# The last two output projections of a two-layer attention kernel: one moved behind the last attention, the last one rebuilt from block and quarter products

## The chip, the cores and the metric

The kernel runs on one core of a Trainium2 chip. The metric is the device time of one execution in microseconds (us). Beside it there is one profiled execution, whose records give the start and length of every instruction on every engine: TensorE (PE, its weight loads PEld), VectorE (DVE), ScalarE (ACT), GpSimd (POOL) and the queue of SyncE (SP), which issues the DMA transfers.

## The reference

Two layers of the same form are applied to x of shape (8, 512, 32, 32), all in float32. With N = 1024 positions and C = 512 channels, for each image:

```python
xn = group_norm(x) * gamma + beta              # 8 groups in layer 0, 32 in layer 1
q, k, v = split(qkv_w @ xn + qkv_b)            # each 512 x 1024, 8 heads of 64
p = softmax(q.T @ k / 8)                       # per head, 1024 x 1024
out = p @ v.T                                  # per head, back to 512 x 1024
x = proj_w @ out + proj_b + x                  # output projection and residual
```

## The kernel before

**Units.** A unit is one image in one layer: units 0 to 7 are layer 0, units 8 to 15 layer 1. For each unit `fast_path` issues, in program order: the q, k and v projections (`projections`), then the output projection of the unit before (`project(old, after)`, L1163), then its own attention (`attention`, L1207). So the softmax tail of a unit is worked off beside the next unit's projections, and its output projection stands between the next unit's projections and attention. Unit 15 has no next unit: its output projection is `project_last` (L759, called in L1220).

**Order.** Nothing is planned by costs: every engine works through its instructions in the order in which the program issues them, and waits are put in by data dependence (and by `gate`, a TensorE instruction that waits for named others). Work of other units is threaded in through numbered calls: in `projections` and `project` every step ends in a call `done`, and a table says which parts are issued at which call.

**Products.** `blocks` (L422) multiplies two 2x2 block matrices with seven block products instead of eight. A block product is four matrix products of 512 columns. For some of the seven, each is made again from seven quarter products of 256 columns (`inner_products`, L437, `mix_inner`, L187). For the output projection, products 2, 3 and 4 are of that kind (`INNER["o"]`), 1, 5, 6 and 7 plain. Each needs sums and differences of blocks of the right operand (`mix_right`, L167), and of the left one, which is prepared once per layer (`left_o`, and for the quarters `inner_left` in DRAM).

The order of one projection, with its `done` calls: product 1, copied by ScalarE to p1 (call 1); product 6, added by VectorE to p1, giving u2 (call 2, in which VectorE also adds bias and residual to u2); quarter group 2, then `c11`, the first result block (call 3); product 7, its sum u3 (call 4, residual into u3); product 5, `others(1,1)` (call 5, residual into p1); quarter group 4, `others(1,0)` (call 6); quarter group 3, `others(0,1)` (call 7). In a quarter group ScalarE copies four of the seven results out of their banks (L460): quarter products 1, 6 and 7 of a group go into one bank one after the other, each one added to the last, and each is copied before the next. GpSimd then sums these copies (`fold`, L466) and adds them to the results (`rests`, L741), which are stored.

**Attention.** 64 steps: 8 chunks (4 pairs of heads by 2 halves of the positions) of 8 steps. A step is eight score products (L820), an exponential on ScalarE (L828) into one of four `p` buffers, a row sum on VectorE (L865, L867) and eight products with v (L848). At the end of a pair the row sums are transposed, reduced and sent through DRAM to become reciprocals `rb` for all rows (`reciprocals`, L901); VectorE multiplies with them (`divide`, L928) and ScalarE adds v's bias (`add_bias`, L935). For the last pair of a unit this lies behind attention.

**The last projection** has none of the mixing: for eight result tiles it multiplies the first three of four pieces (24 products of 512 columns), issues the last pair's reciprocals, division and bias, then the fourth pieces, each followed by one VectorE instruction and a store.

**Buffers.** `ppool` has four buffers `p`, `accpool` two `acc`, `trpool` two `tr`, `tmppool` one `tmp`, `rbpool` one `rb`; TensorE's results are in four two-bank tiles: `sbank[0]`, `sbank[1]` ("s" in the profile), `apair[0]`, `apair[1]` ("a").

Of the kernel before, what the change touches and what calls it, by code (L numbers as in the profile page):

```python
# [11 lines left out]
F32 = mybir.dt.float32  # L12
I32 = mybir.dt.int32
AF = mybir.ActivationFunctionType
ALU = mybir.AluOpType
# [3 lines left out]
P = 128  # L19
# [13 lines left out]
def fast_path(ctx, tc, x, qkv_wT, proj_wT, vecs, groups, out, flag):  # L33
# [55 lines left out]
    turns = [t[:, i, :] for i in range(2) for t in (*sbank, *apair)]  # L89
# [33 lines left out]
    def load_xn(u):  # L123
        t = xnpool.tile([P, CC, N], F32, tag="xn", name=f"xn_{u}")
        load_x(u, [t[:, c, :] for c in range(CC)])
        return t
# [37 lines left out]
            lefts.append({1: a11, 2: a12, 3: s4, 4: a22, 5: s1, 6: s2, 7: a21})  # L164
        return lefts, parts

    def mix_right(name, low, high):  # L167


        b11, b12 = low[:, :, :FD], low[:, :, FD:]  # L170
        b21, b22 = high[:, :, :FD], high[:, :, FD:]
        factors = {1: b11, 2: b21, 3: b22, 7: b12}

        def part(i):
            if i == 0:
                for k, n in ((5, 1), (6, 2), (4, 4)):
                    factors[k] = tpool.tile([P, 2, FD], F32, tag=f"{name[0]}{n}", name=f"{name}_t{n}")
            t1, t2, t4 = (factors[k] for k in (5, 6, 4))
            nc.vector.tensor_sub(
                *((t1, b12, b11), (t2, b22, t1), (t4, b21, t2), (b12, b22, b12))[i]  # L180
            )

        return factors, [partial(part, i) for i in range(4)]
# [77 lines left out]
    def load_proj(l, tag):  # L261
        w = wpool.tile([P, CC, C], F32, tag=tag, name=f"wproj_{l}_{tag}")
        nc.sync.dma_start(w, proj_wT[l].rearrange("(c p) o -> p c o", p=P))
        return w
# [155 lines left out]
                )  # L420

    def blocks(name, left, right, tokens, c11, others, done, u3_in, summed, inner={}, rests=None,  # L422
               u2_in=(trpool, "tr"), between=None, behind=None, p1=None):

# [38 lines left out]
                step(j)  # L463
            return (rest, partial(step, order[-1])) if k == 1 else rest

        def fold(rest):  # L466
            add = nc.gpsimd.tensor_add
            add(rest[:, 0, FD2:], rest[:, 0, FD2:], rest[:, 1, FD2:])  # L468
            add(rest[:, 1, FD2:], rest[:, 1, :FD2], rest[:, 1, FD2:])

        def add_rest(r, h, rest, alone=None):

            if rest is not None:
                fold(rest)
                rests(r, h, rest, alone)
# [52 lines left out]
        done(sums)  # L528
        rest = inner_products(bz, 3)
        others(0, 1, bz, u2, twice)  # L530
        add_rest(0, 1, rest, u2 if twice is not None else None)
        if twice is not None:
            rests(0, 1, twice)
        done(sums)
# [157 lines left out]
        if not w.v_first:  # L692
            values()

    def project(w, after):


        l, b = units[w.u]
# [39 lines left out]
                if (r, h) == (1, 1):  # L738
                    store(o, h)

        def rests(r, h, rest, _):  # L741
            for i in range(2):
                o = 2 * r + i
                cols = results[o, h]
                nc.gpsimd.tensor_add(cols, cols, rest[:, i, :])
                store(o, h)

        w.evac = [None, None]
# [4 lines left out]
        }  # L753
        inner = {k: (*w.inner_o[k], *plan[k]) for k in w.inner_o}
        w.taken = blocks(
            f"o_{w.u}", w.left, w.right_o, False, c11, others, done, (rbpool, "rb"), plain_sum, inner, rests
        )

    def project_last(w, rest):  # L759

        l, b = units[w.u]
        dst = mid[b] if l == 0 else out[b]

        def products(g, c):
            o, h = divmod(g, NH)
            nc.tensor.matmul(  # L766
                turns[g], w.wproj[:, c, ts(o, P)], w.ao[c // 2][:, c % 2, ts(h, FD)],
                start=(c == 0), stop=(c == CC - 1),
            )

        for g in range(CC * NH):
            for c in range(CC - 1):
                products(g, c)
        for part in rest:
            part()
        for g in range(CC * NH):
            o, h = divmod(g, NH)
            products(g, CC - 1)
            cols = w.res[o][:, ts(h, FD)]
            nc.vector.scalar_tensor_tensor(  # L780
                cols, turns[g], vec[:, l, PB, o : o + 1], cols, ALU.add, ALU.add
            )
            nc.sync.dma_start(dst[o * P : (o + 1) * P, ts(h, FD)], cols)

    def attention(w, at_step, at_end):


        u = w.u
        w.ao = [
            aopool.tile([P, 2, N], F32, tag=f"ao{i}", name=f"ao_{u}_{i}") for i in range(2)  # L790
        ]
# [183 lines left out]
        def bias_last():  # L975
            for h in range(NH):
                add_bias(CC - 1, h)

        w.right_o, mixing = mix_right(f"o_{u}", *w.ao)

        parts = {
# [7 lines left out]
        lefts = []  # L989

        def load_left():
            n = 2 * FD // P
# [11 lines left out]
        def mix_o(k):  # L1004
            tag = {2: "x2", 3: "x1", 4: "x4"}[k]
            room = tpool.tile([P, 4, FD2], F32, tag=tag, name=f"ro{k}_{u}")
            if k == INNER["o"][-1]:
                w.inner_o[k] = mix_inner_in(w.right_o[k], room, nc.vector)
                lefts.append(room[:, 3, :P])
                if u == B:  # L1010
                    make_left(2)
                else:
                    nc.sync.dma_start(lefts[-1], src[:, len(lefts) - 1, :])
            else:
                w.inner_o[k], subs = mix_inner(w.right_o[k], room, nc.vector)
                for part in subs:
                    part()
# [10 lines left out]
        w.finish = finish  # L1028
        return parts


    xn = xnpool.tile([P, CC, N], F32, tag="xn", name="xn_0")
    tiles = [xn[:, c, :] for c in range(CC)]
# [33 lines left out]
    for u in range(2 * B):  # L1067
# [54 lines left out]
        if old is not None:  # L1122
            old.res = load_res(old.u)
        nxt = None
        if u + 1 < 2 * B:
            xn = load_xn(u + 1)
            nxt = norm_parts(u + 1, xn)
            right, mixing = mix_right(f"x_{u + 1}", xn[:, :2], xn[:, 2:])
            for transfer in behind_loads:
                transfer()  # L1130
            behind_loads.clear()
        else:
# [70 lines left out]
        def at_end():  # L1203
            if u + 1 < 2 * B:
                w.made_next = load_inner_left(u + 1)

        rest = attention(w, at_step, at_end)  # L1207
        old = w

    both = const.tile([P, 1], F32, name="both")  # L1210
# [10 lines left out]
    nc.tensor.matmul(turns[0][:1, :1], both, ones[:, :1], start=True, stop=True)  # L1221
    nc.scalar.copy(flag, turns[0][:1, :1])


def general_path(ctx, tc, x, qkv_wT, proj_wT, vecs, groups, out):
# [260 lines left out]
```

## Time and profile before

| | us |
|---|---|
| time of the kernel before, median of 3 runs (range) | 3257.72 (3256.99 to 3259.81) |
| span of the profiled execution | 3256.9 |
| TensorE busy | 3244.5 |
| VectorE busy | 2715.3 |
| ScalarE busy | 1650.2 |
| GpSimd busy | 1216.3 |
| end of unit 15's q, k, v projections on the chain | 3089.74 |
| first scores of the last attention | 3112.54 |
| end of the last attention's products | 3222.57 |
| end of the last projection's products | 3250.27 |

A line of a timeline gives the start and the length in us, the engine, the line of the program, the operation, what it writes and reads by the program's names, the shape, and how many such instructions were merged. In brackets stands how long the engine had been idle before, and what ended that. The chain of work that ended last is followed back from the last instruction: at each step to what released it, or to the instruction before it on its engine. A float32 matrix product appears as two records.

### The profile page before, as it was taken

To read this page: it belongs to the slowest core of one execution; us is meant where nothing else is said; L and a number is where in the kernel's file an instruction comes from. 1 tells how busy PE (TensorE), PEld (TensorE's weight loads), DVE (VectorE), ACT (ScalarE), POOL (GpSimd) and SP (SyncE) were. 2 spreads that over 40 slices of the span, in tenths; PEclk is the share of its full clock that TensorE was granted. 3 is DMA by queue.
4 is the path that set the end of the run, shared out by engine and by line. 5 is a ranking of instruction groups with operands and counts; after the bars stand their busy time and mean duration, and the time that the engine had idled before them with its cause. 6 is when DMAs were issued, how large, how long until landed. Compare 5 with 4: busy or idle time off the path is not lost.

```text
span 3256.9 us, 56805 instructions
## 1 busy us (share of the span) xinstructions
PE 3244.5 (100%) x22206; PEld 1863.3 (57%) x22206; DVE 2715.3 (83%) x3488; ACT 1650.2 (51%) x2296; POOL 1216.3 (37%) x1207
## 2 busy tenths in 40 slices
PE   9999999999999999999999999999999999999999
PEld 5465474654746547465574655747556474564743
DVE  5887978789787897989979889797897978979786
ACT  1653626546274463744637446373563735637354
POOL 2054171531706317063270732607126071350710
PEclk9999999999999999999999999999999999999999
DMA  3112120121201212023120121201212012120111
GB/s 104 48 45 79 46 79 28 45 79 46 85 22 45 85 43 86 18 71 114 55 87 27 45 86 46 85 16 45 86 46 85 17 54 76 46 85 22 67 71 48
DMA packets 86463, 192.51 MB, mean 59 GB/s; under 512 B 22960, under 2 KB 34992, under 8 KB 84272
## 3 DMA queue, kind: packets, MB, share of 16 engines
q1 hardware_dynamic: 86192, 188.82, 17.0%
q8 instruction: 180, 2.95, 0.4%
q14 instruction: 91, 0.75, 0.1%
HBM read 148.00 MB, written 39.19 MB: 57 GB/s over the span
## 4 chain that ended last, share of the span: by engine, by line
PE 96%; DVE 3%; issue 0%; DMA 0%; ACT 0%; SPq 0%; DVEq 0%
PE a L848 26%; PE s L820 25%; PE s L416 14%; PE a L416 12%; PE a L455 10%; PE s L455 9%; DVE acc L867 1%; PE a L820 1%; PE s L766 0%; PE a L766 0%; DVE tr L880 0%; PE s L361 0%; DVE acc L865 0%; DVE ao L874 0%; DMA xn<-x_dram 0%
## 5 line engine op out<-in xcount | busy, mean ns | idle before, releaser
L828 ACT ACTIVATE p<-s 128x1024 f32<-128x1024 f32 x976 | 998.0, 1024 | 558.0 <-PE s L820 516.6
L848 PE MATMUL a<-p,v 64*64 64x512 f32 x8192 | 1099.8, 589 | 0.0
L820 PE MATMUL s<-q,k 64*64 64x512 f32 x7808 | 1058.1, 590 | 0.0
L867 DVE TENSOR_TENSOR acc<-acc,p 128x1024 f32<-128x1024 f32 x768 | 968.6, 1261 | 61.7 <-ACT p L828 13.0
L848 PEld LDWEIGHTS a<-p,v 64*64 64x64 f32 x8192 | 383.2, 131 | 495.8 <-ACT p L828 350.2
L820 PEld LDWEIGHTS s<-q,k 64*64 64x64 f32 x7808 | 383.5, 133 | 431.9 <-issue 422.8
L1088 POOL TENSOR_TENSOR r<-xn 128x256 f32<-128x256 f32 x30 | 49.5, 1649 | 1175.7 <-DVE acc L867 1038.3
L650 POOL TENSOR_TENSOR k<-k,m_k 128x512 f32<-128x512 f32 x180 | 259.6, 1463 | 0.0
L865 DVE TENSOR_TENSOR acc<-p,p 128x1024 f32<-128x1024 f32 x128 | 156.2, 1220 | 20.5 <-ACT p L828 13.9
L312 POOL TENSOR_TENSOR y<-var,half 128x4 f32<-128x4 f32 (+1 forms) x17 | 33.2, 1950 | 344.4 <-DVE var L310 344.4
L880 DVE STREAM_TRANSPOSE tr<-acc 128x1024 f32<-128x1024 f32 x128 | 157.9, 1234 | 0.0
L650 POOL TENSOR_TENSOR q<-q,m_q 128x512 f32<-128x512 f32 x120 | 157.2, 1325 | 0.0
L890 DVE TENSOR_REDUCE red<-tr 128x32 f32<-128x1024 f32 x128 | 154.4, 1206 | 0.6
L538 DVE TENSOR_TENSOR u_v<-s,p_v 128x1024 f32<-128x1024 f32 x32 | 39.2, 1224 | 123.7 <-PE s L416 123.7
L501 ACT COPY p_o<-a 128x1024 f32<-128x1024 f32 x15 | 15.2, 1012 | 244.2 <-PE a L416 244.2
L874 DVE TENSOR_TENSOR ao<-a,tmp 128x512 f32<-128x512 f32 x128 | 88.0, 688 | 60.9 <-ACT tmp L873 59.6
L460 ACT COPY m_q<-s 128x256 f32<-128x256 f32 x150 | 55.9, 373 | 145.3 <-PE s L455 142.7
L468 POOL TENSOR_TENSOR m_o<-m_o 128x256 f32<-128x256 f32 x45 | 34.2, 760 | 251.7 <-ACT m_o L460 251.7
L416 PE MATMUL s<-x_t,s2w 128*128 128x512 f32 x256 | 117.5, 592 | 0.0
L416 PE MATMUL a<-w,xn 128*128 128x256 f32 x496 | 112.1, 379 | 0.0
L460 ACT COPY m_k<-s 128x256 f32<-128x256 f32 x165 | 61.5, 373 | 93.8 <-PE s L455 90.2
L334 ACT ACTIVATE xn<-xn,shift,scale 128x512 f32<-128x512 f32 x124 | 99.5, 804 | 10.9 <-DVE shift L330 10.9
(291 smaller groups left out, 5130.5 us busy)
## 6 DMA issues: line engine op xcount, KB each, us to landing
rb<-drec SPq DMA_DIRECT2D x128, 256.0 KB, 3.9
xn<-mid SPq DMA_DIRECT2D x36, 512.0 KB, 7.9
il<-ilk SPq DMA_DIRECT2D x15, 1152.0 KB, 7.0
xn<-x_dram SPq DMA_DIRECT2D x32, 512.0 KB, 7.0
x<-x_dram SPq DMA_DIRECT2D x32, 512.0 KB, 5.5
x<-mid SPq DMA_DIRECT2D x28, 512.0 KB, 4.9
il<-ilq SPq DMA_DIRECT2D x15, 768.0 KB, 4.2
mid<-u_o SPq DMA_DIRECT2D x32, 256.0 KB, 2.1
```

Of the source, the lines that this page charges most:

```text
L334: nc.scalar.activation(cols, cols, AF.Identity, bias=st["shift"][:, c - lo : c - lo + 1], scale=st["scale"][:, c - lo : c - lo + 1],)
L416: nc.tensor.matmul(dst, at[:, c, ts(i, P)], moving[:, c, :], start=start and c == 0 and not (tokens and i % 2), stop=stop and c == 1, skip ...
L455: nc.tensor.matmul(dst[j], a[j], b[j], start=j in (1, 5) or first and j in (2, 4), stop=j not in (1, 6), skip_group_check=True,)
L460: taken.append(nc.scalar.copy(to[j], dst[j]))
L650: w.last[sel].append(add(cols, cols, rest[:, i, :]))
L820: nc.tensor.matmul(bank[e * H : (e + 1) * H, j, :], w.k[pr][j * H : (j + 1) * H, t * P + e * H : t * P + (e + 1) * H], w.q[pr][j * H : (j ...
L828: exp = nc.scalar.activation(p, bank, AF.Exp, scale=SCALE)
L848: nc.tensor.matmul(banks[r][j * H : (j + 1) * H, :], w.v[rows, t, lo : lo + D], p[rows, j, :], start=(t == 0), stop=(t == NT - 1),)
L865: nc.vector.tensor_add(acc, state["first"], p)
L867: nc.vector.tensor_add(acc, acc, p)
L880: nc.vector.transpose(tr, state["acc"].pop(c))
L890: nc.vector.tensor_reduce(red[:, :, qh, :], state["tr"].rearrange("p j (f i) -> p j f i", i=BL), AX.X, ALU.add)
```

## The change

`project(old)` for unit 14 is no longer issued between unit 15's projections and its attention, but behind that attention. `project_last` is gone: unit 15 goes through `project` as well, with the same seven block products, of which three are made of quarters. What unit 15 needs for that is threaded into unit 14's projection: reciprocals at call 2, one mixing at call 3, division and bias at call 5, the other mixings at calls 6 and 7, and the quarter mixings at call 7 and at calls 1 and 2 of unit 15's own projection. The verdict on the row sums comes at its call 3.

Buffers are found for it: unit 15's attention result lies in the buffer of xn, its mixed blocks in `p` buffers, its quarter mixings in v's buffer, unit 14's u3 in a `p` buffer, the left quarter factors (one load for both units) in `w0`, and the residuals are loaded into q and k buffers of head pairs that are finished: four loads at step 36, two at step 52, two behind attention. The second load of xn and of the projection's weights falls away. In unit 15's projection the last `fold` and the last `rests` are on VectorE instead of GpSimd (`end=nc.vector`).

```diff
-    def mix_right(name, low, high):
+    def mix_right(name, low, high, rooms=None):
...
-                    factors[k] = tpool.tile([P, 2, FD], F32, tag=f"{name[0]}{n}", name=f"{name}_t{n}")
+                    factors[k] = rooms[n] if rooms else tpool.tile([P, 2, FD], F32, tag=f"{name[0]}{n}", name=f"{name}_t{n}")
...
-        def fold(rest):
-            add = nc.gpsimd.tensor_add
+        def fold(rest, engine=nc.gpsimd):
+            add = engine.tensor_add
...
-        add_rest(0, 1, rest, u2 if twice is not None else None)
+        if end is nc.gpsimd:
+            add_rest(0, 1, rest, u2 if twice is not None else None)
+        else:
+            fold(rest, end)
+            rests(0, 1, rest, None, end)
...
-    def project(w, after):
+    def project(w, after, u3_in=(rbpool, "rb"), end=nc.gpsimd):
...
-    def project_last(w, rest):
...
+        last = u == 2 * B - 1
+        if last:
+            ao = xnpool.tile([P, CC, N], F32, tag="xn", name=f"ao_{u}")
+            w.ao = [ao[:, 2 * i : 2 * i + 2, :] for i in range(2)]
...
+        if last:
+            return last_parts(w, partial(reciprocals, CC - 1), partial(divide, CC - 1), bias_last)
...
+    def load_left_last():
+
+        n = 3 * len(INNER["o"])
+        t = wpool.tile([P, n, P], F32, tag="w0", name="lo_last")
+        nc.sync.dma_start(t, inner_left[1]["o"].rearrange("p k s o -> p (k s) o"))
+        lefts_last.extend(t[:, i, :] for i in range(n))
+        return lefts_last
+
+    def last_parts(w, reciprocals, divide, bias):
+
+
+        tiles = [ppool.tile([P, 2, FD], F32, tag="p", name=f"o_last_t{n}") for n in (1, 2, 4)]
+        w.right_o, mixing = mix_right("o_last", *w.ao, dict(zip((1, 2, 4), tiles)))
+        flat = vpool.tile([P, NT, C], F32, tag="v", name="ro_last")
+        w.inner_o, subs = {}, {}
+
+        def room(i, k):
+            made, subs[k] = mix_inner(
+                w.right_o[k], flat[:, 2 * i : 2 * i + 2, :].rearrange("p t (s c) -> p (t s) c", s=2), nc.vector
+            )
+            w.inner_o[k] = (inner_lefts(k, w.left[k], lefts_last[3 * i : 3 * i + 3]), made)
+
+        def rooms():
+            for i, k in enumerate(INNER["o"]):
+                room(i, k)
+
+        def subs_of(k):
+            for part in subs[k]:
+                part()
+
+        first = {
+            2: [reciprocals], 3: [mixing[0]], 5: [divide, bias], 6: [mixing[1], mixing[3]],
+            7: [mixing[2], rooms, lambda: subs_of(2)],
+        }
+        return first, {1: [lambda: subs_of(4)], 2: [lambda: subs_of(3)]}
...
-        else:
-
-            again = load_xn(u)
-            w.res = [again[:, c, :] for c in range(CC)]
-            w.wproj = load_proj(1, "w0")
...
+        if old is not None and nxt is not None:
...
             if nxt is None:
+                if s in (4 * NT + 4, 6 * NT + 4):
+                    res_in_qk(s // NT // NH)
                 return
...
+        def res_in_qk(pairs):
+
+            tiles = [
+                qkpool.tile([P, N], F32, tag=tag, name=f"x_{u}_{pairs}_{i}{tag}")
+                for i in range(pairs) for tag in "qk"
+            ][: 4 if pairs == 2 else 2]
+            if pairs == 2:
+                old.res = tiles
+                load_x(old.u, tiles)
+            else:
+                w.res += tiles
+                load_x(u, tiles, len(w.res) - 2)
...
-    project_last(old, [part for g in (3, 10, 14) for part in rest[g]] + [verdict])
+    res_in_qk(1)
+    w.left = left_o
+    first, second = rest
+    second[3] = [verdict]
...
+    project(old, in_order(first), (ppool, "p"))
+    project(w, in_order(second), end=nc.vector)
```

More of the change, by code (lines that the diff above doesn't have):

```diff
@@ L87, in fast_path @@
     abank = [apair[i // 2][:, i % 2, :] for i in range(4)]
-    turns = [t[:, i, :] for i in range(2) for t in (*sbank, *apair)]
     vec = const.tile([P, 2, 6, CC], F32, name="vec")
@@ L422, in blocks @@
     def blocks(name, left, right, tokens, c11, others, done, u3_in, summed, inner={}, rests=None,
-               u2_in=(trpool, "tr"), between=None, behind=None, p1=None):
+               u2_in=(trpool, "tr"), between=None, behind=None, p1=None, end=nc.gpsimd):
         bx, by, bz = apair[0], sbank[0], apair[1]
@@ L739, in others, with rests @@
                     store(o, h)
-        def rests(r, h, rest, _):
+        def rests(r, h, rest, _, engine=nc.gpsimd):
             for i in range(2):
@@ L744, in rests @@
                 cols = results[o, h]
-                nc.gpsimd.tensor_add(cols, cols, rest[:, i, :])
+                engine.tensor_add(cols, cols, rest[:, i, :])
                 store(o, h)
@@ L755, in project @@
         w.taken = blocks(
-            f"o_{w.u}", w.left, w.right_o, False, c11, others, done, (rbpool, "rb"), plain_sum, inner, rests
-        )
-    def project_last(w, rest):
[L761 to L783, printed above, removed]
+            f"o_{w.u}", w.left, w.right_o, False, c11, others, done, u3_in, plain_sum, inner, rests,
+            end=end,
+        )
     def attention(w, at_step, at_end):
         u = w.u
-        w.ao = [
-            aopool.tile([P, 2, N], F32, tag=f"ao{i}", name=f"ao_{u}_{i}") for i in range(2)
-        ]
+        last = u == 2 * B - 1
[3 more added lines that the diff above has]
+        else:
+            w.ao = [
+                aopool.tile([P, 2, N], F32, tag=f"ao{i}", name=f"ao_{u}_{i}") for i in range(2)
+            ]
         n_chunks = CC * NH
@@ L991, in load_left @@
         def load_left():
+            if u == 2 * B - 2:
+                lefts.extend(load_left_last())
+                return
             n = 2 * FD // P
@@ L1008, in mix_o @@
                 w.inner_o[k] = mix_inner_in(w.right_o[k], room, nc.vector)
-                lefts.append(room[:, 3, :P])
+                if len(lefts) < 3 * len(INNER["o"]):
+                    lefts.append(room[:, 3, :P])
                 if u == B:
                     make_left(2)
-                else:
+                elif u < 2 * B - 2:
                     nc.sync.dma_start(lefts[-1], src[:, len(lefts) - 1, :])
@@ L1029, in attention @@
         return parts
+    lefts_last = []
+    def load_left_last():
[25 more added lines that the diff above has]
+        return first, {1: [lambda: subs_of(4)], 2: [lambda: subs_of(3)]}
     xn = xnpool.tile([P, CC, N], F32, tag="xn", name="xn_0")
@@ L1121, in fast_path @@
         between = None
-        if old is not None:
+        if old is not None and u + 1 < 2 * B:
             old.res = load_res(old.u)
@@ L1131, in fast_path @@
             behind_loads.clear()
-        else:
-            again = load_xn(u)
-            w.res = [again[:, c, :] for c in range(CC)]
-            w.wproj = load_proj(1, "w0")
         left_parts = {}
@@ L1205, in at_end @@
                 w.made_next = load_inner_left(u + 1)
+        def res_in_qk(pairs):
[6 more added lines that the diff above has]
+                load_x(old.u, tiles)
+            else:
+                w.res += tiles
+                load_x(u, tiles, len(w.res) - 2)
+        w.res = []
         rest = attention(w, at_step, at_end)
+        if nxt is None:
+            break
         old = w
@@ L1218, in verdict, with in_order, after @@
         nc.vector.tensor_mul(both, low[:, 0:1], low[:, 1:2])
-    project_last(old, [part for g in (3, 10, 14) for part in rest[g]] + [verdict])
-    nc.tensor.matmul(turns[0][:1, :1], both, ones[:, :1], start=True, stop=True)
-    nc.scalar.copy(flag, turns[0][:1, :1])
+    res_in_qk(1)
+    w.left = left_o
+    first, second = rest
+    second[3] = [verdict]
+    def in_order(parts):
+        def after(g):
+            for part in parts.get(g, ()):
+                part()
+        return after
+    project(old, in_order(first), (ppool, "p"))
+    project(w, in_order(second), end=nc.vector)
+    nc.tensor.matmul(sbank[0][:1, 0, :1], both, ones[:, :1], start=True, stop=True)
+    nc.scalar.copy(flag, sbank[0][:1, 0, :1])
 def general_path(ctx, tc, x, qkv_wT, proj_wT, vecs, groups, out):
```

## The prediction

> **What bounds the kernel now.** I read the page's engine totals first, then the chain of work that ended last over the last 200 us, then the timelines of single engines at both edges of the last attention. Totals:
>
> ```profile
> PE 3244.5 (100%) x22206; PEld 1863.3 (57%) x22206; DVE 2715.3 (83%) x3488; ACT 1650.2 (51%) x2296; POOL 1216.3 (37%) x1207
> ```
>
> TensorE is never free, so time is won only by fewer products, and every new gap on TensorE costs its full length. The chain (start, length, what):
>
> ```profile
> 3086.29 6.89 PE a L416 x24
> 3093.17 3.43 PE s L416 x8
> ...
> 3112.54 1.88 PE s L820 x16
> ...
> 3219.99 2.58 PE a L848 x24
> 3222.57 5.35 PE s L766 x12
> ...
> 3248.51 1.73 PE a L766 x4
> 3250.27 0.75 DVE xn L780
> ```
>
> Projections of unit 15 end at 3089.74 (16 of the 24 records, 3.45 us, are theirs), projection of unit 14 fills TensorE to 3112.54, attention 15 runs to 3222.57 (110.03), the last projection to 3250.27 (27.70), and one VectorE tail of 0.75 follows. There is no gap at any border. VectorE at the first border and in projection 14 (start, length, line):
>
> ```profile
> 3089.78 1.22 DVE L675 TENSOR_TENSOR v<-a,u_v 128x1024 f32<-128x1024 f32 x1 [2.23 <-PE a L416]
> 3090.92 1.22 DVE L179 TENSOR_TENSOR ao<-ao,ao 128x1024 f32<-128x1024 f32 x1
> ...
> 3095.91 0.42 DVE L1017 TENSOR_TENSOR ro<-ao,ro 128x256 f32<-128x256 f32 x1
> 3096.74 1.23 DVE L538 TENSOR_TENSOR u_o<-s,p_o 128x1024 f32<-128x1024 f32 x1 [0.42 <-PE s L416]
> 3098.00 1.42 DVE L703 SCALAR_TENSOR_TENSOR u_o<-x,vec,u_o 128x512 f32<-128x512 f32 x2
> ...
> 3106.59 1.29 DVE L737 TENSOR_TENSOR u_o<-a,u_o 128x512 f32<-128x512 f32 x2 [0.81 <-PE a L416]
> ```
>
> Seen there: the last v is ready at 3091.00, 1.26 after TensorE finished it, and the prices of the projection's steps. The last attention's end, timeline of all engines:
>
> ```profile
> 3230.15 0.54 DVE L913 RECIPROCAL rec<-rows 32x64 f32<-32x64 f32 x1
> ...
> 3236.63 1.22 DVE L930 SCALAR_TENSOR_TENSOR ao<-ao,rb 128x1024 f32<-128x1024 f32 x1 [5.62 <-DMA rb<-drec]
> ...
> 3237.89 1.33 ACT L937 ACTIVATE ao<-ao,vec 128x512 f32<-128x512 f32 x2 [13.45 <-DVE ao L930]
> ```
>
> Reciprocals travel through DRAM for 5.94 us (3230.69 to 3236.63), then divide, then two bias instructions on ScalarE. Today ScalarE waits 13.45 us there with nothing queued behind it that TensorE needs.
>
> **What the Trainium skill says.** "Perfetto Trace Analysis", section "Tensor Engine Instruction (MATMUL, LD_WEIGHTS)": ScalarE, VectorE and GpSimd are strict FIFO. The trace agrees: each engine's instructions start in program order, and ScalarE sat through those 13.45 us. "SBUF — State Buffer", section "Who interferes with whom": a VectorE instruction with two SBUF inputs blocks against a GpSimd one that reads SBUF. The trace agrees: the L179 subtraction takes 1.22 alone and up to 2.11 (at 3075.20, beside GpSimd's L650); L1017 takes 0.42 alone, 0.94 beside it. "TensorE: Matmul & The Clock Gate", section "What's actually happening": after an idle window of about 3.4 us, free-running, the array runs at half clock until a window has been busy. The trace fits at its start:
>
> ```profile
> 4.47 2.93 PE L361 MATMUL s<-xn 128*128 128x256 f32 x6 [4.47 <-DMA xn<-x_dram]
> ```
>
> That is 0.49 each, against 0.215 for records of 256 columns later.
>
> **The change part by part** (t counts from the end of attention's products, 3222.57 now).
>
> *Products.* The last projection has 32 products of 512 columns, two records of 0.43 each: 27.5, on the chain 27.70. In the new form, priced from projection 14 in this trace, there are four block products (8 records, 3.43) and three quarter groups (14 records of 256 columns, 3.01): 22.75. So -4.95. Projection 14 keeps its 22.8 and only moves.
>
> *Start of attention 15.* Its first scores wait for all of v, since no projection stands between any more. v is ready at 3091.00, TensorE free at 3089.74; with about 0.14 to pass the wait, +1.4 (1.3 to 1.8). Behind the waiting scores the whole queue of TensorE stands. VectorE's mixing for projection 14 then runs to 3096.33, while exponentials arrive: first row sums about 2 us late. They take 1.26 a step against TensorE's 1.72, and four p buffers bridge it: 0. Without that cover it would be those 2 us.
>
> *Transfers.* Gone before attention: 2 MB of xn again and 1 MB of weights. The 2 MB residual of unit 14 moves to step 36, 1 MB of unit 15's to step 52, the other 1 MB behind the row-sum transfers after attention; the left factors become one 576 KB load. SP issues four loads in 1.81 us; the rb transfer issued behind them has 8 steps (13.7 us) and needs about 6. Cost 0; were rb later than 13.7, VectorE would be late by the rest.
>
> *Projection 14 behind attention.* Its operands are ready, its first bank (a) was freed by the exponential ending 3221.14: no gap at t=0. TensorE: products 1, 6, quarter group 2, products 7, 5 end at 3.43, 6.86, 9.87, 13.30, 16.73. VectorE, by the pitches of those rows, starts its sum at 6.99 and is then never idle: sum 1.26, residual into u2 1.33, reciprocals 1.86, c11 1.33, first mixing 1.5 (beside GpSimd), sum 1.26, residual 1.33: 16.86; two adds 1.20, residual into p1 1.33: 19.39; divide 1.22: 20.61. rb is there: reciprocal done 11.1 plus 5.94 is 17.1, 2.3 early; a later rb adds its excess.
> The bias pair is put at this point (done call 5), ahead of quarter group 4's copies on ScalarE. It ends at 20.65+1.33 = 21.98. Group 4's first copy stands behind it, until 22.35; its fourth product adds into the bank that copy reads, so it starts at 22.45. TensorE reaches that product at 16.73+1.29 = 18.02. **+4.4**. Nothing in the before trace has this wait: bounds 0 (if the copy does not stand behind the bias) and 5.2 (mixing at 2.1 and 0.2 of waits). I take 4.4, because FIFO order decides it.
>
> *Projection 15.* With the stall, group 4 ends 24.17, group 3 27.18; then 30.61, 34.04, group 2 37.05. VectorE: adds to 25.5, two mixings 28.5, adds 29.7, third mixing 31.2, eight subtractions for groups 2 and 4 (L1017's mean, 0.72, pitch) to 37, sum 38.2. Product 7 at 37.05 reuses the bank that this sum reads: I take +0.5; bounds 0 (subtractions at 0.36) and 3.9 (mixings 2.1, subtractions 0.87: sum ends 41). After that VectorE is nearer, and the verdict's 0.8 hides in it.
>
> *Tail.* The final fold and adds go to VectorE after the last product: 0.13 wait, two adds 1.20, two folds of 128x256 (0.36 to 0.87 each, I take 0.6), two adds of 128x512 with SBUF inputs (no undisturbed row: half of 1.22 below, 0.88 as in the L578 row of that size above; 0.68 taken): 3.9, against 0.75 now: +3.1 (2.5 to 4.0). The last store follows at once in both.
>
> Sum: -4.95+1.4+4.4+0.5+3.1 = +4.45. The profiled execution spans 3256.9, its runs have a median of 3257.7; I add the sum to the latter: **3262.2**.
>
> **Rivals.**
> A (forecast): saving eaten by the FIFO stall and the longer tail, +4.45.
> B, the saving shows: the bias stall does not happen, since divide comes early or the copy is not held. -4.95+1.4+0+0+2.5 to 3.1 = about -1, 3256.7. For it: in projection 14 now VectorE has idle time (2.36 before its second sum). Against: reciprocals, mixing and divide add 5.8 us to that queue.
> C, slower beyond the bound: the clock gate. Place: the fourth product of group 4. If a free-running 3.4 us window falls wholly inside the 4.4 us gap, the following products run at half clock for at least one window: 1.7 to 3.4 us more, +6.2 to +7.9, about 3264.8. It decides as soon as the gap passes 3.4 with the window aligned: at 4.4, 1.0/3.4 = 3 in 10, more if rb is late too. For it: 0.49 at the start after 4.47 idle. Against: PEclk reads 9 throughout.
> D: the change saves nothing since the left factors or residuals arrive late. Loads land in 5 to 8 us, against tens of us ahead; under 2 in 100.
>
> **How the numbers follow.** 0.2% is 6.5 us, about what a measurement of this kernel can tell from no change; the whole saving is under it, so faster needs an effect that I don't see: 0.02. A 0.56, of which 0.04 passes +6.5 by its upper bounds; C 0.27, nearly all of it above; B 0.14; the rest 0.03. Slower 0.30, same 0.68. A alone: 3259.5 to 3264.5. The range runs from B (3256.5) to C with some port blocking (3267).
>
> **What would show it.** Right: a gap near 1.4 before the first scores of attention 15; ScalarE's L937 followed at once by an m_o copy, and TensorE waiting some 4 us for ScalarE in projection 14; 3 to 5 us of VectorE after the last product. Wrong: no gap there (B); matmul records at twice their length behind it (C); product 7 of the last projection waiting for VectorE by more than 2 us (port blocking).

## The result and the profile after

| | before | after |
|---|---|---|
| time, median of 7 runs each (range), us | 3257.99 (3256.99 to 3259.93) | 3268.78 (3267.07 to 3269.17) |
| span of the profiled execution, us | 3256.9 | 3267.0 |
| end of the last unit's projections, us | 3089.74 | 3091.07 |
| end of the last attention (E), us | 3222.57 | 3202.77 |
| last matrix product ends, us | 3250.27 | 3257.86 |
| last VectorE instruction ends, us | 3251.02 | 3261.56 |

The ratio after to before is 1.003, with a 95% interval of 1.0019 to 1.004. The changed kernel, run again in eight runs on the chip of the last experiments, had 3267.16 against 3258.47: 1.0026 (1.0016 to 1.0037). So the change costs 9 to 11 us. 3262.2 was forecast, and the range ended at 3267: the time lies above it.

TensorE's total on the page after looks as it did before; VectorE's is 23 us larger (busy us, share of the span, instructions):

```profile
PE 3244.6 (99%) x22216; PEld 1874.4 (57%) x22216; DVE 2738.3 (84%) x3516; ACT 1654.5 (51%) x2309; POOL 1223.4 (37%) x1215
```

TensorE is busy for as long as before, although the last projection has 4.95 us less of products to do. Busy time is counted by the clock on the wall: products that run slower count more. The place must be read from the edges.

The chain of work that ended last, of the kernel after, at the start of the last attention (start, length, what):

```profile
3087.60 3.47 PE a L414 x16
3091.07 0.02 issue
3091.09 1.24 DVE v L677
3092.32 0.35 issue
3092.68 1.95 PE s L802 x16
```

TensorE stands still for 1.6 us between the last projection product and the first scores, with VectorE's last v in between. (That this border comes 1.33 us later than before has arisen at the program's start: the chain there runs through a load of x that took 4.68 us, where before it ran through one of 3.68. Nothing that the change touches lies there.) The same view from the end of the attention and unit 14's projection on (E stands for the end of attention's products):

```profile
3200.20 2.58 PE a L830 x24
...
3223.49 1.24 DVE ao L912 x2
3224.75 0.04 ACT ao L919
3224.80 0.58 issue
3225.38 0.70 ACT ao L919
3226.08 0.26 ACT m_o L458
3226.35 0.04 issue
3226.39 1.22 PE a L453 x2
...
3235.07 1.81 DVE o_last_t L177
...
3237.78 4.00 DVE ro_last L1051 x4
...
3258.77 1.07 DVE m_o L466
...
3261.12 0.44 DVE u_o L747
```

Two things stand there. In the middle is the predicted chain: divide (L912), the bias pair (L919), one copy (L458), then the quarter product that adds into the copied bank (L453). Around it the chain runs over VectorE, where before it was TensorE to the end. The waits of the kernel after from 3196 on (engine, what waits for what: us in total, times, longest):

```profile
ACT ao L919 <- DVE ao L912: 11.5, 1, 11.5
...
PE a L453 <- ACT m_o L458: 5.4, 1, 5.4
...
DVE p_o L739 <- PE s L453: 4.6, 1, 4.6
```

ScalarE sits in its queue for VectorE's division, TensorE for the copy behind it, VectorE for the product behind that. TensorE's timeline shows the products on both sides of its wait (start, length of the merged group, shape, count, idle before):

```profile
3220.43 0.59 PE L453 MATMUL s<-o_t,lo_last 128*128 128x256 f32 x2
3226.39 1.22 PE L453 MATMUL a<-ro,lo_last 128*128 128x256 f32 x2 [5.37 <-ACT m_o L458]
3227.41 1.06 PE L453 MATMUL s<-ro,lo_last 128*128 128x256 f32 x2
...
3232.29 0.59 PE L453 MATMUL s<-ro,lo_last 128*128 128x256 f32 x2
```

A pair that took 0.59 with the time to drain takes 1.06 to 1.22 behind the wait, for some 5.5 us. The granted clock confirms it (stretch, busy us and instructions of PE, PEld, DVE, ACT and POOL, then PEclk, share of DMA, GB/s):

```profile
3220.80:3226.30 5.50, 0.22 (x2) 0.00 (x0) 3.92 (x7) 1.55 (x3) 0.00 (x0) 0.90 0.38 144
3226.30:3229.70 3.40, 3.31 (x8) 2.68 (x9) 0.34 (x1) 0.78 (x3) 0.68 (x1) 0.50 0.00 0
3229.70:3233.10 3.40, 3.40 (x12) 2.79 (x11) 3.40 (x4) 0.93 (x3) 2.42 (x3) 0.66 0.00 0
3233.10:3236.50 3.40, 3.40 (x11) 1.93 (x11) 3.06 (x4) 0.94 (x3) 3.40 (x3) 1.00 0.20 77
```

0.50, 0.66, then 1.00. The records put the half clock at 6.83 us in all. TensorE did 8 and 12 instructions where 16 fit in 3.4 us, and lost 2.75 us. In the third and fourth stretch VectorE is busy all but 0.34 us, and GpSimd all but 0.98. VectorE's own timeline (start, length, line, shape, idle before) has long instructions in it:

```profile
3212.53 0.74 DVE L889 TENSOR_TENSOR one<-red,lt 32x64 f32<-32x64 f32 x1
...
3231.70 1.75 DVE L177 TENSOR_TENSOR ao<-ao 128x1024 f32<-128x1024 f32 x1
...
3234.99 1.90 DVE L177 TENSOR_TENSOR o_last_t<-ao,o_last_t 128x1024 f32<-128x1024 f32 x1
...
3238.53 1.49 DVE L1051 TENSOR_TENSOR ro_last<-ao 128x256 f32<-128x256 f32 x1
...
3242.47 0.42 DVE L1051 TENSOR_TENSOR ro_last<-o_last_t,ro_last 128x256 f32<-128x256 f32 x1
```

The same L177 subtraction takes 1.22 alone, L1051 takes 0.42 in the last line and 1.49 four us earlier, and L889, an addition of only 32x64, 0.74 instead of 0.21.

**The sum in spans.** Before, E to the last VectorE instruction held 27.70 + 0.75 = 28.45, and with the 22.80 of the moved projection it would be 51.25. After, it is 3261.56 - 3202.77 = 58.8, so 7.55 more:

| term | us |
|---|---|
| products of the last projection | -4.95 |
| stall in group 4 (TensorE arrives 3220.86, starts 3226.39) | +5.5 |
| half clock behind it | +2.75 |
| waits of 0.2 and 0.5 in unit 15's projection | +0.7 |
| tail on VectorE (3.7 instead of 0.75) | +2.95 |
| not placed | +0.6 |

With the gap of 1.6 ahead of the attention, the 1.33 from the program's start and 0.4 less behind the last VectorE instruction, that is the 10.1 between the spans.

### The profile page after: what moved, and what is told of

It reads as the page before. It is cut to its first block, busy times and chain, and to the rows that moved or that the text cites. A ratio compares the mean times of both kernels' runs of the same rounds, so it can differ in the third digit from the quotient of the medians.

```text
span 3267.0 us, 56882 instructions
## 1 busy us (share of the span) xinstructions
PE 3244.6 (99%) x22216; PEld 1874.4 (57%) x22216; DVE 2738.3 (84%) x3516; ACT 1654.5 (51%) x2309; POOL 1223.4 (37%) x1215
## 3 DMA queue, kind: packets, MB, share of 16 engines
q8 instruction: 180, 2.95, 0.4%
## 4 chain that ended last, share of the span: by engine, by line
PE 97%; DVE 2%; issue 0%; DMA 0%; ACT 0%; SPq 0%; DVEq 0%
PE a L830 27%; PE s L802 26%; PE s L414 13%; PE a L414 12%; PE a L453 10%; PE s L453 8%; PE a L802 1%; DVE acc L849 0%; PE s L359 0%; DVE ro_last L1051 0%; DVE u_o L540 0%; DMA xn<-x_dram 0%; DVE u_o L705 0%; DVE u_o L739 0%; DVE o_last_t L177 0%
## 5 line engine op out<-in xcount | busy, mean ns | idle before, releaser
L849 DVE TENSOR_TENSOR acc<-acc,p 128x1024 f32<-128x1024 f32 x768 | 967.0, 1259 | 61.5 <-ACT p L810 12.7
L458 ACT COPY m_q<-s 128x256 f32<-128x256 f32 x150 | 55.8, 372 | 145.2 <-PE s L453 142.6
L458 ACT COPY m_k<-s 128x256 f32<-128x256 f32 x165 | 61.4, 372 | 93.8 <-PE s L453 90.3
```

The source lines that it names most:

```text
L458: taken.append(nc.scalar.copy(to[j], dst[j]))
L849: nc.vector.tensor_add(acc, acc, p)
```

## The experiments

Two theories were set against each other. T: TensorE's own losses (gap, stall, half clock) make the excess; take them away and each comes back in full. V: behind the attention VectorE's queue is the bound as soon as the stall has put it late, stretched by GpSimd's adds beside it; time given back to TensorE turns into new waits for VectorE. Ratios are to the kernel before on the same chip, with 95% intervals. "E to end" is from the end of attention's products to the end of the last VectorE instruction; the kernel before, with the moved projection added, has 51.25 there.

| run | median us | before | ratio | E to end, us |
|---|---|---|---|---|
| e0_after | 3267.16 | 3258.47 | 1.0026 (1.0016 to 1.0037) | 58.3 |
| e1_bias_later | 3264.10 | 3258.10 | 1.0017 (1.0010 to 1.0024) | 54.6 |
| e2_keep_busy | 3264.96 | 3258.10 | 1.0021 (1.0013 to 1.0030) | 56.7 |
| e3_gate | 3265.94 | 3258.10 | 1.0023 (1.0014 to 1.0031) | 58.2 |
| e4_move_alone | 3259.63 | 3258.10 | 1.0004 (0.9996 to 1.0012) | 51.3 |
| e5_plain | 3266.24 | 3258.43 | 1.0024 (1.0014 to 1.0034) | 55.9 |
| e6_plain_early_gate | 3258.97 | 3258.43 | 1.0002 (0.9994 to 1.0011) | 50.2 |
| e7_quarters_early_gate | 3262.32 | 3258.43 | 1.0012 (1.0006 to 1.0019) | 54.7 |
| e8_early | 3264.15 | 3258.43 | 1.0016 (1.0009 to 1.0023) | 55.2 |
| e9_best | 3258.36 | 3258.47 | 1.0000 (0.9991 to 1.0008) | 49.2 |
| e10_no_gpsimd | 3259.91 | 3258.47 | 1.0004 (0.9996 to 1.0013) | 50.9 |

### The changed kernel again (e0_after)

No edit; it stands beside the last runs, on their chip.

> The changed kernel once more, unaltered, on the same chip as the two others: 3267 to 3269, with 10 more than the kernel before.

Measured +8.7. The wait for ScalarE has the same place and length (5.37), and product 7 of unit 15's projection waits 0.95 for VectorE's sum, which was 0.2 in the first profile. The half clock again lasts 6.83, but 3.1 us of it fall into the wait itself: the products from there to the end of group 3 take 6.7 us, where they took 7.6 in the first profile and take 4.85 at the full clock (e2). So it costs some 1.85 here and not 2.75.

### Is the half clock the wait's doing? (e2_keep_busy)

Six products without use go into the wait, into a bank that is free there.

```diff
+                if name == "o_14" and k == 4 and j == 3:
+                    for _ in range(6):
+                        nc.tensor.matmul(
+                            sbank[1][:, 1, :], left[1][:, 0, :P], right[1][:, 0, :], start=True, stop=True
+                        )
```

> Six added products of 512 columns (5.15 us, their result is used by nothing) stand ahead of the fourth product of quarter group 4 in projection 14, where TensorE waited 5.4 us; the bias stays where the change put it. If the clock gate made the following records slow, they take 0.43 a pair again: theory T expects 2.7 us less than the changed kernel (3266.1), theory V 1.2 us less (3267.6), because only the three slow products ahead of the adds of call 6 delay VectorE. If the slow records have another cause (operands, banks), they stay at 0.86 a pair and the time stays at 3268.8.

TensorE's timeline:

```profile
3224.85 0.70 PE L453 MATMUL a<-ro,lo_last 128*128 128x256 f32 x2 [0.23 <-ACT m_o L458]
3225.39 0.59 PE L453 MATMUL s<-ro,lo_last 128*128 128x256 f32 x2
...
3240.98 3.70 PE L414 MATMUL s<-ao,wproj_wproj 128*128 128x512 f32 x8 [1.23 <-DVE u_o L545]
```

The product behind the wait starts no earlier relative to the division, but the pairs are back at 0.59 to 0.70 and the clock reads 1.0 to the end. So an idle TensorE, and nothing in the operands, made the products slow. E to end falls by 2.1 against the first profile (58.8), where the half clock had cost 2.75, and by 1.6 against the second (58.3), where it had cost 1.85; product 7 now waits 1.23 for VectorE. The median is 2.2 under e0_after, on another chip.

### The bias later in ScalarE's queue (e1_bias_later)

```diff
-            2: [reciprocals], 3: [mixing[0]], 5: [divide, bias], 6: [mixing[1], mixing[3]],
+            2: [reciprocals], 3: [mixing[0]], 5: [divide], 6: [bias, mixing[1], mixing[3]],
```

> The last bias goes from call 5 to call 6, so that quarter group 4's copies stand ahead of it on ScalarE. Both theories expect the 5.4 us wait of TensorE in projection 14 and the half-speed records behind it to be gone. Theory V (from that wait on, VectorE's queue sets the end, it is idle for only 4.6 us there and almost never after): 4.6 us less than the changed kernel, about 3264.2, with VectorE without a gap to the end and TensorE waiting for VectorE in projection 15. Theory T (TensorE stays the bound, as the prediction summed it): 5.5 of wait and 2.7 of half speed come back whole, 8.2 less, about 3260.6. Theory W (the wait is not ScalarE's order): no change.

The time is what V gave, but not by V's way: both theories took the wait as gone, and it was not. It moved one quarter group on:

```profile
3225.37 0.70 PE L453 MATMUL s<-ro,lo_last 128*128 128x256 f32 x2 [3.35 <-ACT m_o L458]
```

Now group 3's copies stand behind the bias pair, which is still waiting for the late division. One half-clock stretch of 3.41 us follows. Wait and half clock are both smaller, 3.35 and 3.41 instead of 5.37 and 6.83, and the time is 3.1 under e0_after, on another chip (E to end: 3.7 less). The stall belongs to the late division; where the bias is queued only decides which copies pay.

### The division earlier (e8_early)

```diff
-            2: [reciprocals], 3: [mixing[0]], 5: [divide, bias], 6: [mixing[1], mixing[3]],
+            1: [reciprocals], 3: [divide, bias], 5: [mixing[0]], 6: [mixing[1], mixing[3]],
```

> Only the order in projection 14 changes: reciprocals at call 1 instead of 2, division and bias at call 3 instead of 5, first mixing at call 5 instead of 3, so that the bias is through ScalarE before the first copy of quarter group 4. Unlike with the bias at call 6, where TensorE still waited 3.35 us in group 3, no wait of TensorE on ScalarE is left in projection 14 and the clock stays at 1.0. Theory V (VectorE's queue sets the end in the last projection): the last VectorE instruction ends about 54 us behind attention's end instead of 58.8, the time is 4.8 less than the changed kernel, about 3264, and TensorE waits for VectorE at product 7 of the last projection. Theory T (TensorE stays the bound): 5.5 of wait and 2.7 of half speed come back, about 3260.6.

The stall is gone (0.55 is left in group 4, for a bank), and if T held, 5.5 + 2.75 would have come back. 3264.15 is what V gave: 3 come back. TensorE's timeline has a new wait instead, for VectorE, and VectorE's timeline shows why:

```profile
3219.98 0.70 PE L453 MATMUL s<-o_t,wproj_wproj 128*128 128x256 f32 x2 [0.55 <-DVE u_o L540]
...
3236.69 0.67 PE L453 MATMUL s<-ro_last,lo_last 128*128 128x256 f32 x2 [2.17 <-DVE ro_last L1051]
```

```profile
3227.15 1.91 DVE L177 TENSOR_TENSOR o_last_t<-ao,o_last_t 128x1024 f32<-128x1024 f32 x1
3228.99 2.28 DVE L177 TENSOR_TENSOR ao<-ao 128x1024 f32<-128x1024 f32 x1
3231.19 1.28 DVE L739 TENSOR_TENSOR u_o<-a,u_o 128x512 f32<-128x512 f32 x2
3232.39 1.35 DVE L177 TENSOR_TENSOR o_last_t<-ao,o_last_t 128x1024 f32<-128x1024 f32 x1
3233.66 1.48 DVE L1051 TENSOR_TENSOR ro_last<-ao 128x256 f32<-128x256 f32 x1
3235.18 1.37 DVE L1051 TENSOR_TENSOR ro_last<-ao,ro_last 128x256 f32<-128x256 f32 x1
3236.47 0.41 DVE L1051 TENSOR_TENSOR ro_last<-ao 128x256 f32<-128x256 f32 x1
```

VectorE works without a pause from one subtraction to the next, so it sets the end although the stall is gone. Those that read two SBUF operands take 1.35 to 2.28 instead of 1.22, and 1.37 to 1.48 instead of 0.42; L739, which reads one operand from TensorE's bank, stays at 1.28. Behind the new wait one stretch at half clock (3.41 us) follows again: the pairs from 3237.19 on take 0.92 to 1.06.

### VectorE without GpSimd beside it (e10_no_gpsimd)

To e8_early's edit is added that GpSimd leaves out its sums of the copied quarters of groups 4 and 3 in unit 14's projection, and their addition to the results:

```diff
-                fold(rest)
+                if name != "o_14" or (r, h) == (0, 0):
+                    fold(rest)
...
-                engine.tensor_add(cols, cols, rest[:, i, :])
+                if w.u != 14 or (r, h) == (0, 0):
+                    engine.tensor_add(cols, cols, rest[:, i, :])
```

> The kernel with early division (quarters kept), but in projection 14 the folds and adds of quarter groups 4 and 3 on GpSimd are left out, so unit 14's output lacks parts of those two groups. VectorE's own instructions stay the same. If GpSimd's reads beside VectorE's two-input subtractions stretch these (1.75 to 2.28 where 1.22 is their undisturbed length, 1.4 where 0.42 is), they go back to 1.22 and 0.42 and the last projection gets its operands about 4 us earlier: TensorE's 2.2 us wait in group 2 and the half-speed records behind it go, about 3 less than the kernel with early division, 3261. If the stretch has another cause, the durations and the time (3264.2) stay.

Measured 3259.91, 4.2 less than e8_early, more than was expected. Its VectorE timeline:

```profile
3224.91 1.21 DVE L177 TENSOR_TENSOR o_last_t<-ao,o_last_t 128x1024 f32<-128x1024 f32 x1
3226.04 1.22 DVE L177 TENSOR_TENSOR ao<-ao 128x1024 f32<-128x1024 f32 x1
...
3229.50 0.42 DVE L1053 TENSOR_TENSOR ro_last<-ao 128x256 f32<-128x256 f32 x1
```

The durations are back at 1.22 and 0.42, the wait of 2.17 is absent, and the clock stays at 1.0. (A subtraction beside a GpSimd sum that was left in still takes 0.94.) E to end is 50.9 instead of 55.2. So GpSimd's adds, for which no instruction of TensorE or VectorE waits, cost some 4 us by stretching VectorE's work beside them. In e8 they show as about 2.5 us of waits of TensorE and 1.7 of half clock; e7 below, with the same wait but without that half clock, still has 54.7. A second effect goes with them: a copy to p1 that an output store had held for 6.05 us is free. In e8 it delayed TensorE by 0.3 us, ahead of the wait for VectorE. "SBUF — State Buffer", section "Who interferes with whom", in the Trainium skill names this pair (a VectorE instruction with two SBUF inputs against a GpSimd one that reads SBUF); the runs agree and give the size.

### The gap before the attention (e3_gate)

The first scores wait only for the earlier parts of v, the third for its last part.

```diff
-                before = before + w.last["q"] + (w.evac_before[:1] or w.last["v"])
+                v = w.last["v"][:-1] if u == 2 * B - 1 else w.last["v"]
+                before = before + w.last["q"] + (w.evac_before[:1] or v)
...
+                if u == 2 * B - 1:
+                    before = before + w.last["v"][-1:]
```

> The first scores of attention 15 wait for all of v but its last quarter; the third scores, whose bank that last addition reads, wait for it. Both theories expect the gap of 1.6 us ahead of attention to close: 1.6 less than the changed kernel, about 3267.2. If the gap has another cause, the first scores start as late as before and nothing changes.

```profile
3090.34 1.95 PE L805 MATMUL s<-q,k 64*64 64x512 f32 x16
```

The first scores start with no idle time ahead of them. The median is 1.2 under e0_after on another chip and 2.8 under the first measurement; 1.6 was expected, and lies between. The profile shows the gap gone, while the two comparisons only bracket its size.

### The move alone (e4_move_alone)

Projection 14 stands behind the attention as in the change, but unit 15's projection is the old one, with its 32 products and its own load of the weights. Division and bias come at call 7.

```diff
+    def project_last(w, rest):
...
+        for g in range(CC * NH):
+            for c in range(CC - 1):
+                products(g, c)
+        for part in rest:
+            part()
...
+        return {2: [reciprocals], 7: [divide, bias]}, {}
```

> Projection 14 stays behind attention 15, but the last projection is the one of the kernel before (32 products, one VectorE instruction each); the last reciprocals stand at call 2, division and bias behind call 7, so no copy waits for the bias. If the move itself costs only the gap ahead of attention: 1.6 us above the kernel before, about 3259.6, no wait of TensorE behind attention, last VectorE instruction 0.75 after the last product. If the moved loads, or VectorE behind attention, cost as well: 3 us or more above it, with TensorE waiting in projection 14 or at the border.

3259.63, as expected, 1.5 above before: the gap (TensorE's timeline) is all that the move itself costs.

```profile
3090.90 1.95 PE L830 MATMUL s<-q,k 64*64 64x512 f32 x16 [1.63 <-DVE v L679]
```

Behind the attention TensorE never waits, and E to end is 51.25, to the digit what the kernel before has with the moved projection added. So moving the projection and its loads is nearly free, and the rest of the loss comes from what was threaded into it for the new last projection.

### Seven block products without quarters (e5_plain, e6_plain_early_gate, e7_quarters_early_gate)

e5_plain lets unit 15's projection use its seven products whole and leaves the bias where it was. In e5 and e6 three of those products still take left factors in which one quarter had been replaced in place by the quarter form's difference: their work is that of whole products, their result is not the reference's.

```diff
-            7: [mixing[2], rooms, lambda: subs_of(2)],
+            7: [mixing[2]],
...
-        return first, {1: [lambda: subs_of(4)], 2: [lambda: subs_of(3)]}
+        return first, {}
...
-    project(w, in_order(second), end=nc.vector)
+    project(w, in_order(second))
```

> The changed kernel with seven plain block products in the last projection: no quarter groups there, so 1.3 us more TensorE work, and 12 subtractions, 6 folds, 8 adds of rests and 12 copies fewer; the wait for the bias in projection 14 stays. Theory V: the last projection becomes TensorE's again, its end lies 1.4 behind its last product instead of 3.7, 56.6 behind attention's end instead of 58.8, so about 2.2 less than the changed kernel (3266.6). Theory T, where the subtractions cost nothing and only TensorE's work and the tail count: 1.3 - 2.3 = 1.0 less (3267.8).

It is 0.9 under e0_after, on another chip, with the half clock at 6.83 us as before. That is too close to both numbers to tell V from T. E to end tells more: it is 2.4 shorter than in e0_after, where V gave 2.2 and T 1.0. The median hides it, since 6.9 us instead of 5.5 pass behind the last VectorE instruction.

e6 adds to this the early division (e8) and the gate (e3); e7 has early division and gate with the quarters kept.

> Plain block products in the last projection, division and bias early as in e8, and the first scores' wait without v's last quarter. No wait of TensorE from attention 15 to the end: 22.8 + 24.0 of products behind attention and 1.4 of tail, 48.1, and no gap ahead of attention. Against the kernel before: 24.0 + 1.4 in the place of 27.7 + 0.75, so 3.1 less than it, about 3255.0. If VectorE or the clock still intervenes, it is at the kernel before or above.

> The change as it was meant, quarters kept, with division and bias early and the loosened wait of the first scores: theory V expects e8 less the 1.6 us gap, about 3262.4, above the kernel before by 4; theory T about 3259.

e7 came as V said (3262.4), not as T did (3259). Its TensorE timeline, set against that of e8_early, shows the clock from another side:

```profile
3234.97 0.67 PE L453 MATMUL s<-ro_last,lo_last 128*128 128x256 f32 x2 [2.18 <-DVE ro_last L1054]
...
3235.91 0.59 PE L453 MATMUL a<-ro_last,wproj_wproj 128*128 128x256 f32 x2
```

The wait is e8_early's (2.18 and 2.17), but the pairs behind it take 0.59 here and up to 1.06 there. Whether a wait of this length costs a slow stretch depends on when it falls. In each execution the changes of the clock lie whole multiples of 3.41 us apart, so the time can be cut into pieces of that length (stretch, length, busy us and instructions of PE, PEclk, share of DMA, GB/s; e8_early first, then e7):

```profile
3233.92:3237.33 3.41, 1.24 (x6) 1.00 0.26 100
3237.33:3240.74 3.41, 3.36 (x8) 0.50 0.15 56
...
3230.37:3233.78 3.41, 2.28 (x8) 1.00 0.00 0
3233.78:3237.19 3.41, 1.97 (x8) 1.00 0.41 154
```

In e8_early the whole wait falls into one piece, which leaves TensorE 1.24 us of work in it, and the next piece runs at half clock. In e7 a border divides the wait, and both pieces stay above that. The two executions differ by 1.7 us of half clock, but by only 0.5 in E to end: VectorE's queue is the bound in both.

e6 missed: 3258.97 instead of 3255.0. In its profile E to end is 50.2 instead of the 48.1 expected, and 6.7 us pass behind the last VectorE instruction where before has 5.9; together that is 2.9 of the miss. Two waits of TensorE stand behind the first part. In the loads' order, residual loads stood ahead of the reciprocals' trip: from the issue of the reciprocals' store to that of rb's load 2.73 us passed, 1.36 before, and TensorE waited 0.65 in group 4. And a copy to p1 was held 6.04 us by an output store, for which TensorE then waited 0.56. The rest of the 4 us was not placed.

### The best that the runs pointed to (e9_best)

Whole products, early division, the gate, residual loads behind the reciprocals, p1 in v's buffer, the left quarters restored with one subtraction each, and one mixing moved into the last projection. Its output is the reference's.

```diff
+                v = w.last["v"][:-1] if u == 2 * B - 1 else w.last["v"]
+                before = before + w.last["q"] + (w.evac_before[:1] or v)
...
+        def whole(k):
+            a11, a21 = w.left[k][:, 0, :P], w.left[k][:, 0, P:]
+            nc.vector.tensor_sub(a21, a11, a21)
...
-            2: [reciprocals], 3: [mixing[0]], 5: [divide, bias], 6: [mixing[1], mixing[3]],
-            7: [mixing[2], rooms, lambda: subs_of(2)],
+            1: [reciprocals], 3: [divide, bias], 5: [lambda: whole(2), mixing[0]], 6: [mixing[1], mixing[3]],
+            7: [lambda: whole(4)],
...
-        return first, {1: [lambda: subs_of(4)], 2: [lambda: subs_of(3)]}
+        return first, {2: [lambda: whole(3), mixing[2]]}
...
-    res_in_qk(1)
...
+    first[2] = [lambda: res_in_qk(1)]
...
-    project(w, in_order(second), end=nc.vector)
+    project(w, in_order(second), p1_in=(vpool, "v"))
```

> The plain last projection with early division and loosened first wait, and with the two waits closed that were left in it: the residuals behind attention are loaded after the reciprocals' trip instead of ahead of it (rb about 1.4 us earlier, so the 0.65 us wait in group 4 goes), and p1 of the last projection lies in v's buffer instead of one that is still being stored (0.7 us). Three subtractions of 128x128 bring back the left quarters that the quarter form had replaced, so that plain products can use them. Expected: 22.8 + 24.0 + 1.45 behind attention, no wait of TensorE, 2.5 to 3 less than the kernel before, about 3255.5; if VectorE or the start of the program takes it back, 3258.

A tie: 1.0000 (0.9991 to 1.0008). Behind the attention TensorE's timeline has a single wait left, 0.24 in group 4. From the attention's start to the last VectorE instruction it takes 159.2 us, against 161.28 before (138.48 and the 22.80 of projection 14, which stood ahead): 2.1 are won. Behind that instruction 7.2 us pass until the span ends, against 5.9 before; the last two stores took 4.3 us to land instead of 2.8. e5 and e6, whose last projection is whole as well, have 6.9 and 6.7 there. Why was not followed up, so where the expected 2.5 to 3 us went is settled only in part: 1.3 of them lie behind the last instruction of any engine.

## Why the prediction was wrong

*Products, gap, tail, transfers: right.* The saving of 4.95 is in the sum, and the gap (1.4 forecast, 1.6 measured; e4 shows it alone, e3 takes it away) and the tail (3.9 forecast, 3.7 measured) were near. (The row L578, by which the tail's last adds were bounded with 0.88, is one of 128x256 and not "of that size"; the 0.68 taken was near all the same, a pair took 1.29.) No load was late for an operand in the changed kernel, so D fell.

*The stall: mechanism right, size short.* The bias pair does stand ahead of group 4's copy in ScalarE's queue, and e1 and e8 show that the late division is its cause. 5.5 instead of 4.4: the division ended 21.94 after E instead of 20.61. Two additions of 32x64 among the reciprocals' instructions were priced undisturbed (0.21) and took 0.74 and 0.76 beside GpSimd, the mixing 1.85 instead of 1.5.

*The step that failed: "+4.4" was counted as the length of the gap alone,* with the clock left standing in the likeliest case. C had the mechanism, the place and the price (3.4 us at half clock cost 1.7, two stretches up to 3.4), but a chance of 0.27, reasoned from a gap just above 3.4. At 5.5 the same reasoning gives (5.5 - 3.4)/3.4, about 6 in 10, so the short gap also made the chance short. After, e0, e3 and e5 show the slow clock behind their wait, e2 shows that the idle time causes it. Nor did the condition hold that an idle window must fall wholly inside the gap: in e0 the clock fell behind a piece with 2.3 us of idle time, in e8 with 2.2. A gap of 4.4, however it falls on pieces of 3.41, leaves at least 2.2 in one of them, so by these runs (an estimate) the slow clock was near certain and belonged into case A. The Trainium skill's "TensorE: Matmul & The Clock Gate", section "What's actually happening", has gap and slow window as the prediction told them. What it does not lead one to expect is that the clock also fell behind idle times of less than a window: 3.35 in e1 and 2.17 in e8.

*A term that came near by luck: "Product 7 ... I take +0.5".* By the prediction's own list VectorE's sum ends at 38.2 and product 7 is there at 37.05, which is 1.15, and no reason is given for 0.5. Measured, product 7 waited only 0.2, because stall and half clock had brought TensorE there 4.1 late (41.13 after E) and VectorE's sum 3.1 late (41.26). VectorE's list itself was near: from the end of group 4's adds to that sum it took 13.4 us, where 12.7 were forecast.

*The step of B that failed: "+0" for VectorE once the stall is away.* The prediction priced VectorE's queue only behind the stall. e8 and e7 are the case without the stall: TensorE waits 2.2 us for L1051 subtractions of up to 1.48, and e10 puts the price of the stretched VectorE work at 4.2, half clock included. In the changed kernel this is hidden, since TensorE is itself held back by stall and slow clock; that is why taking the stall away (e8) gives back about 3, and not the 5.5 and the half clock behind it.

*In numbers.* From the forecast's +4.45: gap +0.2, stall +1.1, half clock +2.75, waits +0.2, tail -0.2, not placed +0.6, which is +9.1; program start and end (+1.33 and -0.4, in this pair of executions alone) make 10.0. B, which lacked the stall, fell. C's 3264.8 was the closest of the cases, and still short: the longer stall (+1.1), the 0.6 not placed and, in the first measurement, the program's start came on top.

## What to carry to other kernels

When small side work (a bias, a division) moves in between products, list for each engine what stands behind it in the queue: here two ScalarE instructions of 0.7 us each, waiting for a late division, held TensorE for 5.5. A wait of TensorE of some 2 us or more has to be priced with the slow products that can follow (here 5.5 became 8.3), in the likeliest case and not as a rival. And when TensorE gets less to do, price VectorE's queue with the durations it has beside GpSimd's adds; in e8, with the stall gone, the saving of 4.95 was less than the 4.2 of that stretch and the 2.95 of the longer tail.

## What the runs showed of the hardware beyond expectation

- The stretches at half clock between two at full clock come in whole pieces: 6.83 us (2 x 3.41) in after, e0_after and e5_plain, 3.41 in e1, e3 and e8, and none in e2, e4, e6, e7, e9 and e10. In the thirteen profiled executions each of the 19 pieces at full clock in which TensorE was busy for at most 1.49 of 3.41 us (that one in e1) was followed by one at half clock; with 1.66 (e3) or more none was. A full window of idle time was not needed.
- A half-clock piece was followed by a second one where TensorE was busy for 2.23 us of it (after) or less, and by the full clock with 3.21 (e3) or more. So the same wait of 5.37, falling differently on the pieces, slowed the products behind it for 5.6 us in after, 3.8 in e0_after and 3.2 in e3.
- Beside GpSimd's adds even a VectorE addition of 32x64 grew from 0.21 to 0.74, and a subtraction of 128x256 from 0.42 to 1.49; a pair of instructions with one operand each in TensorE's banks kept its 1.28.
- Loads issued just ahead on the same queue lengthened the reciprocals' way through DRAM: 2.73 us between its two issues in e6, 1.36 before, and 1.44 in e9, where those loads stand behind.
